# Cross-attention over 32 batches: the first four batches of x added, measured and normalised one at a time, the second quad added by DMA, early turns of x behind scores

## The chip, the cores and the metric

The kernel runs on one NeuronCore of a Trainium2 chip. Such a core has five engines that run their own instruction queues in order and wait for one another through semaphores: TensorE (matrix products and transposes; PE in the profile, PEld its weight loads), VectorE (DVE), ScalarE (ACT), GpSimd (POOL) and SyncE (SP, which here only issues DMAs). The metric is the device time of one execution in microseconds (us).

## The reference

The inputs are x and ctx, both (32, 256, 256) in fp32, and the weights of two layers. What is computed, cut to what matters:

```python
# layer 0: 16 heads of 16 columns; only batch 0 of the attention is used
att  = softmax(heads(x[0] @ Wq.T) @ heads(ctx[0] @ Wk.T).T / 4) @ heads(ctx[0] @ Wv.T)
x    = x + att                            # the one (256, 256) result is added to all 32 batches
# layer 1, for each batch
nX   = layernorm(ctx) * w1 + b1
nF   = layernorm(x) * w2 + b2
a    = softmax(nF @ nX.T / 16) @ nX       # cross-attention
c    = gelu(a @ fc1.T + fc1_b) @ fc2.T + fc2_b      # through 4 hidden columns
n    = layernorm(c) * w3 + b3
s    = softmax(n @ n.T / 16) @ n          # self-attention
out  = nF + gamma2 * (c + gamma1 * s)
```

## The kernel before, in words

The 32 batches are worked in eight quads of four (QB = 4). A batch is kept as 128 partitions x 2 rows x 256 columns (NC = 2 rows of tokens on a partition). All of x stays in one tile, x_all; ctx comes quad by quad into tiles cq. The order of all instructions is written out by hand: the kernel's Python emits them one after the other, each engine takes its own in the order in which they were emitted, and an instruction that waits holds all that stand behind it on its engine.

First comes layer 0 in eleven calls of head_step (L527, up to about 52 us), with the preparation of ctx for quads 0 and 1 beside it: statistics (stats_c), moments (moments_c), normalisation (norm_c, on GpSimd) and transposes (turn_c). Its result is att (L404, VectorE).

Then layer 1 needs, for each batch n of x:

- **addition** of att: a VectorE addition (L638) for batches 0 to 7, in add_and_stats, or for a whole quad a DMA that accumulates into x_all, issued from GpSimd (add_attention, L561);
- **statistics** of the two rows on VectorE (stats_x, BATCH_NORM_STATS2, L188);
- **moments** (L190): on GpSimd, from the statistics of several rows at once, seven small instructions and one power of -1/2 (L203), which give the scale rs and the shift nmr;
- **normalisation** in place (norm_x, L259): row 0 on GpSimd (L262), row 1 on ScalarE (L264);
- **turn** (turn_x, L568): four transposes on TensorE (L179), then two copies with scale and bias on ScalarE (L572), which give nfT;
- **score** (cross_scores, L585): eight products on TensorE (L590), their maximum on VectorE (L598), two exponentials on ScalarE (L601), which give e.

Before the loop the first eight batches get their additions and statistics (L641 to L657), with three sets of moments on GpSimd (batches 0 and 1, 2 and 3, 4 to 7) between them; values and values_turned make g_sl, which later weighs the attention, from quads 0 and 1 of ctx. Then first_step (L682) runs once for every step s, one batch a step: it transposes the exponentials of batch s - 2 (cross_turned), takes the statistics of x 8 batches ahead and of ctx 12 ahead, makes the moments of a quad of x and the next quad of ctx together at the quad's last step (moments_both), turns x of batch s + 1, normalises x of batch s + 4, turns and normalises ctx of batches s + 4 and s + 8, and makes the score of batch s. Four calls of add_attention (quads 4 to 7) stand at the first step of a quad; two (quads 2 and 3) stand before the loop. From step 20 on the second half of layer 1 is mixed in.

## Time and profile before

| | |
|---|---|
| times of three runs | 259.34, 260.54, 263.97 us; median 260.54 |
| profiled execution | 260.04 us, its span (first to last instruction) 258.3 us |
| mean granted TensorE clock | 0.967 |
| busy, share of the span | TensorE 88%, VectorE 67%, ScalarE 56%, GpSimd 72% |
| chain that ended last, by engine | TensorE 63%, GpSimd 15%, VectorE 12%, ScalarE 3% |
| 52 to 60 us | TensorE 4.86 of 8.00 us busy, VectorE 7.80, ScalarE 3.65, GpSimd 6.97 |
| 60 to 68 us | TensorE 7.23, VectorE 7.62, ScalarE 3.34, GpSimd 7.31; clock 0.79 |
| 68 to 76 us | TensorE 6.17, VectorE 3.35, ScalarE 6.03, GpSimd 7.57; clock 0.79 |
| 92 to 130 us | TensorE 38.00 of 38.00 us, VectorE 28.29, ScalarE 27.93, GpSimd 37.05 |

The busy shares are means over stages that differ. The chain of work that ended last is followed back from the last instruction: at each step it names what released it, so it tells which engine set the pace in which stretch. A row of the timeline gives the start and the length of an instruction (or of several alike), its engine, line and tiles, and in brackets how long the engine had been idle before it and what it waited for. A busy TensorE isn't TensorE at its peak: with half the clock the same products take longer.

### The profile page before, as it was taken

The page shows a single profiled execution, that of the slowest core. Times are in us where ns is not written, and L with a number is a line of the kernel's source. Part 1 is how long each engine was busy: PE and PEld are TensorE (multiplying, and loading weights), DVE is VectorE, ACT ScalarE, POOL GpSimd, SP SyncE. Part 2 cuts the span into 40 slices and gives each one's busy share as a digit, 9 for nine tenths or more (in the row PEclk, how much of TensorE's full clock was granted, in tenths as well). Part 3 has the DMA queues.
Part 4 walks back from the last instruction along what each step waited for, and adds up shares of the span by engine and source line. Part 5 has one row for each costly group of instructions (what it writes and reads, how often), then busy time and mean ns, then how long its engine had stood idle before and what let it go on. Part 6 is the DMA issues. An engine that isn't in the chain of part 4 may idle for free.

```text
span 258.3 us, 4919 instructions
## 1 busy us (share of the span) xinstructions
PE 226.9 (88%) x1797; PEld 167.3 (65%) x1797; DVE 171.8 (67%) x371; ACT 144.4 (56%) x297; POOL 185.6 (72%) x298
## 2 busy tenths in 40 slices
PE   3878989977699999999999999989999699899960
PEld 3655666645487787978888796666666356565530
DVE  1369669799738587776868565465445567877482
ACT  1126454444686787677858984656743655454610
POOL 7006827989999989999958989992419808999200
PEclk9999999997979999999999999999999979999995
DMA  6859997059398766718000000000000024343466
GB/s 204 279 190 381 384 388 278 4 100 192 63 241 221 125 202 114 213 28 141 0 3 0 0 3 0 4 0 0 0 3 0 4 81 162 123 159 132 161 237 256
DMA packets 17526, 32.76 MB, mean 127 GB/s; under 512 B 1175, under 2 KB 2142, under 8 KB 17502
## 3 DMA queue, kind: packets, MB, share of 16 engines
q1 hardware_dynamic: 12462, 23.28, 24.8%
q0 software_dynamic: 3168, 6.29, 14.7%
q10 hardware_dynamic: 1872, 2.88, 3.1%
q8 instruction: 14, 0.23, 0.4%
q14 instruction: 10, 0.08, 0.1%
HBM read 17.73 MB, written 8.39 MB: 101 GB/s over the span
## 4 chain that ended last, share of the span: by engine, by line
PE 63%; POOL 15%; DVE 12%; ACT 3%; issue 3%; DMA 1%; DVEq 0%; ACTq 0%; POOLq 0%
PE sc L590 19%; PE sc L368 9%; PE pt_x L179 5%; PE pt_c L179 4%; PE pt_e L179 4%; PE pv L282 3%; PE pu L282 3%; PE po L368 3%; POOL rs_x L203 2%; POOL r L777 2%; PE pf L282 2%; PE pp L321 2%; POOL cq L255 2%; PE ph L282 2%; DVE x_all L934 1%
## 5 line engine op out<-in xcount | busy, mean ns | idle before, releaser
L590 PE MATMUL sc<-nxT,nfT 128*128 128x256 f32 x256 | 64.3, 396 | 0.3 <-ACT nfT L572 0.3
L590 PEld LDWEIGHTS sc<-nxT,nfT 128*128 128x128 f32 x256 | 47.9, 197 | 11.5 <-issue 4.9
L598 DVE TENSOR_REDUCE nm<-sc 128x2 f32<-128x512 f32 x32 | 22.1, 691 | 37.1 <-PE sc L590 20.7
L601 ACT ACTIVATE e<-sc,nm 128x256 f32<-128x256 f32 x64 | 26.8, 470 | 26.1 <-DVE nm L598 26.1
L581 POOL TENSOR_TENSOR x_all<-x_all,w_bc 128x512 f32<-128x512 f32 x32 | 39.6, 1275 | 0.0
L572 ACT ACTIVATE nfT<-pt_x,bq,wq 128x256 f32<-128x256 f32 x64 | 33.3, 582 | 0.0
L179 PE MATMUL pt_x<-ident,x_all 128*128 128x128 f32 x132 | 21.3, 287 | 8.4 <-DMA x_all<-in_x_dram 4.3
L255 POOL TENSOR_SCALAR cq<-cq,rs_b,nmr_b 128x256 f32<-128x256 f32 x40 | 24.8, 708 | 0.0
L188 DVE BATCH_NORM_STATS2 st<-x_all 128x6 f32<-128x256 f32 x64 | 23.9, 415 | 0.3
L179 PEld LDWEIGHTS pt_x<-ident,x_all 128*128 128x128 f32 x132 | 16.2, 147 | 9.4 <-POOL wkT L153 4.2
L179 PE MATMUL pt_e<-ident,e 128*128 128x128 f32 x128 | 20.0, 276 | 2.6 <-ACT e L601 2.5
L356 ACT ACTIVATE e_h<-sc_h,nm_h 128x256 f32<-128x256 f32 x32 | 12.6, 475 | 17.1 <-DVE nm_h L351 17.1
L179 PE MATMUL pt_c<-ident,cq 128*128 128x128 f32 x132 | 20.5, 280 | 1.6 <-DVE ut L801 0.8
L275 DVE COPY nxT<-pt_c 128x512 f32<-128x512 f32 x28 | 19.0, 677 | 4.1 <-PE pt_c L179 4.1
L368 PE MATMUL po<-w_out,vt 32*128 32x256 f32 x128 | 17.9, 412 | 3.4 <-DVE vt L808 2.2
L934 DVE TENSOR_TENSOR x_all<-po,x_all 128x512 f32<-128x512 f32 x26 | 16.7, 684 | 6.0 <-PE po L368 4.2
L188 DVE BATCH_NORM_STATS2 st<-cq 128x6 f32<-128x256 f32 x56 | 20.7, 411 | 0.0
L179 PEld LDWEIGHTS pt_e<-ident,e 128*128 128x128 f32 x128 | 15.4, 141 | 7.3 <-ACT e L601 3.9
L608 ACT COPY eTq<-pt_e 128x512 f32<-128x512 f32 x32 | 18.7, 587 | 1.9 <-PE pt_e L179 1.8
L368 PE MATMUL sc<-tt,ut 32*128 32x256 f32 x128 | 19.4, 403 | 0.0
L368 PE MATMUL sc<-ut 32*128 32x256 f32 x128 | 19.4, 413 | 0.0
L179 PEld LDWEIGHTS pt_c<-ident,cq 128*128 128x128 f32 x132 | 15.5, 143 | 3.6 <-DVE ut L801 1.0
(190 smaller groups left out, 464.9 us busy)
## 6 DMA issues: line engine op xcount, KB each, us to landing
out_dram<-x_all SPq DMA_DIRECT2D x16, 512.0 KB
x_all<-in_x_dram SPq DMA_DIRECT2D x6, 1024.0 KB
x_all<-att POOLq DMA_DIRECT2D x6, 1024.0 KB, 9.2
cq<-in_ctx_dram SPq DMA_DIRECT2D x5, 1024.0 KB
cq<-in_ctx_dram ACTq DMA_DIRECT2D x2, 1024.0 KB
x_all<-in_x_dram SPq DMA_DIRECT2D x1, 1792.0 KB
cq<-in_ctx_dram SPq DMA_DIRECT2D x1, 768.0 KB
wq_nat<-in_L_xattn_Wq_dram ACTq DMA_DIRECT2D x1, 256.0 KB
```

Source lines behind the costliest of these rows:

```text
L179: nc.tensor.transpose(pt[:, dc, t * P : (t + 1) * P], src[:, t, dc * P : (dc + 1) * P], ident)
L188: nc.vector.bn_stats(st[:, t, :], src[:, t, :])
L255: nc.gpsimd.tensor_scalar(row, row, rs[:, i + t, :], nmr[:, i + t, :], ALU.mult, ALU.add)
L275: copy(nxT_of[q][:, b], turned(cq_of[q][:, b], "tp", f"c_{n}"))
L282: nc.tensor.matmul(pg[SL * b : SL * (b + 1), 0, :], weights(kc, b), moving[:, b, kc, :], start=(kc == 0), stop=(kc == NC - 1),)
L368: nc.tensor.matmul(dst[i][:, t, :], lhs[r : r + SL, t * P : (t + 1) * P], rhs[r : r + SL, :], start=True, stop=True,)
L572: nc.scalar.activation(nfT_of[n][:, dc, :], px[:, dc, :], AF.Identity, bias=bq[:, dc : dc + 1], scale=wq2[:, dc : dc + 1],)
L581: nc.gpsimd.tensor_mul(x_all[:, n], x_all[:, n], w2_bc.unsqueeze(1).to_broadcast([P, NC, D]))
L590: nc.tensor.matmul(sc[:, qt, :], nfT[:, dc, qt * P : (qt + 1) * P], nxT[:, dc, :], start=(dc == 0), stop=(dc == NC - 1),)
L598: nc.vector.tensor_reduce(nm, sc, AX.X, ALU.max, negate=True)
L601: nc.scalar.activation(e[:, qt, :], sc[:, qt, :], AF.Exp, bias=nm[:, qt : qt + 1])
L934: nc.vector.tensor_add(x_all[:, n], po[i], x_all[:, n])
```

## The change

The first eight batches are prepared in another way. For batches 0 to 3, add_first does one batch at a time: addition, statistics, then five of the seven small instructions of the moments on VectorE, the power on GpSimd, the statistics of one batch of ctx (11 to 14) on VectorE, and the last two small instructions (product) on VectorE again. Both rows of these four batches are normalised on ScalarE. Batches 4 to 7 are added by DMA (add_attention of the second quad, the first after att), and their statistics and moments come in steps 1 and 2 of the loop, two batches at a time, with the small instructions on VectorE too. Those of batches 8 to 11 come in step 3. The DMA addition of quad 2 stands behind batch 0, those of quads 3 and 4 in steps 0 and 1. In steps 0 to 2 the turn of the next batch of x stands behind the score on TensorE, and ahead of the maximum and the exponentials; the copy of the turn of c7 on ScalarE stands behind the rows of batch 1. From step 4 on the steps are as before.

```diff
@@ -187,28 +187,35 @@
         for t in range(NC):
             nc.vector.bn_stats(st[:, t, :], src[:, t, :])
 
-    def moments(st, n, name):
-
+    def moments(st, n, name, eng=None):
+
+        eng = eng or nc.gpsimd
 
         def t(what, c=1, bufs=2):
             return small.tile([P, n, c], F32, tag=f"{what}{n}", name=f"{what}_{name}", bufs=bufs)
 
         sm, df, sq, v4, ve, nm = t("sm", 2), t("df"), t("sq"), t("v4"), t("ve"), t("nmean")
         rs, nmr = t("rs", 1, 3), t("nmr", 1, 3)
-        nc.gpsimd.tensor_sub(df, st[:, :, 1:2], st[:, :, 4:5])
-        nc.gpsimd.tensor_add(sm, st[:, :, 1:3], st[:, :, 4:6])
-        nc.gpsimd.tensor_mul(sq, df, df)
-        nc.gpsimd.tensor_scalar(v4, sm[:, :, 1:2], 4.0 / D, 4 * EPS, ALU.mult, ALU.add)
-        nc.gpsimd.tensor_add(ve, v4, sq)
+        eng.tensor_sub(df, st[:, :, 1:2], st[:, :, 4:5])
+        eng.tensor_add(sm, st[:, :, 1:3], st[:, :, 4:6])
+        eng.tensor_mul(sq, df, df)
+        eng.tensor_scalar(v4, sm[:, :, 1:2], 4.0 / D, 4 * EPS, ALU.mult, ALU.add)
+        eng.tensor_add(ve, v4, sq)
         nc.gpsimd.tensor_tensor(
             rs.rearrange("p n o -> p (n o)"),
             ve.rearrange("p n o -> p (n o)"),
             neg_half[:, 0:n],
             ALU.pow,
         )
-        nc.gpsimd.tensor_scalar(nm, sm[:, :, 0:1], -0.5, 0.0, ALU.mult, ALU.add)
-        nc.gpsimd.tensor_mul(nmr, nm, rs)
-        return rs, nmr
+
+        def product():
+            eng.tensor_scalar(nm, sm[:, :, 0:1], -0.5, 0.0, ALU.mult, ALU.add)
+            eng.tensor_mul(nmr, nm, rs)
+
+        if eng is nc.gpsimd:
+            product()
+            return rs, nmr
+        return rs, nmr, product
 
     neg_half = const.tile([P, 2 * TQ], F32)
     nc.gpsimd.memset(neg_half, -0.5)
@@ -240,6 +247,16 @@
         rn = moments(flat(st_of[q][:, 1, lo:hi]), (hi - lo) * NC, f"x{q}_{lo}")
         for b in range(lo, hi):
             mx_of[q * QB + b] = *rn, (b - lo) * NC
+
+    def first_moments(lo, hi):
+
+        q, a, b = lo // QB, lo % QB, (hi - 1) % QB + 1
+        rs, nmr, product = moments(
+            flat(st_of[q][:, 1, a:b]), (hi - lo) * NC, f"x{q}_{a}", nc.vector
+        )
+        for n in range(lo, hi):
+            mx_of[n] = rs, nmr, (n - lo) * NC
+        return product
 
     def moments_both(q):
 
@@ -258,12 +275,14 @@
 
     def norm_x(n):
         rs, nmr, i = mx_of.pop(n)
-        row = x_all[:, n, 0, :]
-        nc.gpsimd.tensor_scalar(row, row, rs[:, i, :], nmr[:, i, :], ALU.mult, ALU.add)
-        row = x_all[:, n, 1, :]
-        nc.scalar.activation(
-            row, row, AF.Identity, bias=nmr[:, i + 1, :], scale=rs[:, i + 1, :]
-        )
+        for t in range(NC):
+            row = x_all[:, n, t, :]
+            if t == 0 and n >= QB:
+                nc.gpsimd.tensor_scalar(row, row, rs[:, i, :], nmr[:, i, :], ALU.mult, ALU.add)
+            else:
+                nc.scalar.activation(
+                    row, row, AF.Identity, bias=nmr[:, i + t, :], scale=rs[:, i + t, :]
+                )
 
 
     nxT_of, nfT_of, col_of, eT_of, e_of = {}, {}, {}, {}, {}
@@ -594,12 +613,16 @@
                     start=(dc == 0),
                     stop=(dc == NC - 1),
                 )
-        nm = small.tile([P, NC], F32, tag="nm", name=f"nm_{n}")
-        nc.vector.tensor_reduce(nm, sc, AX.X, ALU.max, negate=True)
-        e = wk.tile([P, NC, D], F32, tag="e", name=f"e_{n}", bufs=6)
-        for qt in range(NC):
-            nc.scalar.activation(e[:, qt, :], sc[:, qt, :], AF.Exp, bias=nm[:, qt : qt + 1])
-        e_of[n] = e
+
+        def softmax():
+            nm = small.tile([P, NC], F32, tag="nm", name=f"nm_{n}")
+            nc.vector.tensor_reduce(nm, sc, AX.X, ALU.max, negate=True)
+            e = wk.tile([P, NC, D], F32, tag="e", name=f"e_{n}", bufs=6)
+            for qt in range(NC):
+                nc.scalar.activation(e[:, qt, :], sc[:, qt, :], AF.Exp, bias=nm[:, qt : qt + 1])
+            e_of[n] = e
+
+        return softmax
 
     def cross_turned(n):
         q, b = n // QB, n % QB
@@ -631,36 +654,31 @@
         nc.vector.tensor_copy(n_all[:, q], g[:, :, :, 0:NM])
 
 
-    for q in range(2, 4):
-        add_attention(q * QB, (q + 1) * QB)
-
-    def add_and_stats(n):
+
+    def add_first(n):
         nc.vector.tensor_add(x_all[:, n], x_all[:, n], att)
         stats_x(n)
-
-    add_and_stats(0)
-    add_and_stats(1)
-    moments_x(0, 0, 2)
+        ends = first_moments(n, n + 1)
+        stats_c(11 + n)
+        ends()
+
+    add_attention(QB, 2 * QB)
+    add_first(0)
     turn_c(4, nc.scalar.copy)
     turn_c(5, nc.scalar.copy)
     values(0)
-    add_and_stats(2)
-    add_and_stats(3)
     turn_c(6, nc.scalar.copy)
+    norm_x(0)
+    add_attention(2 * QB, 3 * QB)
+    add_first(1)
+    values_turned(0)
+    turn_x(0)
+    norm_x(1)
     turn_c(7, nc.scalar.copy)
-    values_turned(0)
-    norm_x(0)
-    norm_x(1)
-    moments_x(0, 2, 4)
     values(1)
-    for n in range(4, 8):
-        add_and_stats(n)
-    turn_x(0)
+    add_first(2)
+    norm_x(2)
     values_turned(1)
-    norm_x(2)
-    norm_x(3)
-    stats_c(11)
-    moments_x(1, 0, 4)
     moments_c(2)
     l0_stage.close()
     late = ctx.enter_context(tc.tile_pool(name="late", bufs=1, reuse_waits="tile"))
@@ -683,23 +701,34 @@
         q, b = s // QB, s % QB
         if b == 0 and 2 <= q and q + 4 < NQ:
             load_c(q + 4)
-        if b == 0 and q + 4 < NQ:
+        if s < 2:
+            add_attention((3 + s) * QB, (4 + s) * QB)
+        elif b == 0 and q + 4 < NQ:
             add_attention((q + 4) * QB, (q + 5) * QB)
         if 0 <= s - 2 < B:
             cross_turned(s - 2)
-        if s + 2 * QB < B:
+        if 0 < s < QB:
+            lo, hi = ((4, 6), (6, 8), (8, 12))[s - 1]
+            for n in range(lo, hi):
+                stats_x(n)
+            if s < QB - 1:
+                first_moments(lo, hi)()
+        elif s >= QB and s + 2 * QB < B:
             stats_x(s + 2 * QB)
-        if s + 3 * QB < B:
+        if s == 2:
+            stats_c(15)
+        elif s >= QB and s + 3 * QB < B:
             stats_c(s + 3 * QB)
         if b == QB - 1 and q + 2 < NQ:
             if q + 3 < NQ:
                 moments_both(q + 2)
             else:
                 moments_x(q + 2, 0, QB)
-        if s + 1 < B:
+        if QB - 1 <= s < B - 1:
             turn_x(s + 1)
-        if s + QB < B:
-            norm_x(s + QB)
+        for n in {0: (), 1: (3,), 2: (4, 5), 3: (6, 7)}.get(s, (s + QB,)):
+            if n < B:
+                norm_x(n)
         if s + QB < B and s >= QB:
             turn_c(s + QB)
         if s + 2 * QB < B:
@@ -720,7 +749,12 @@
         for f, *args in between:
             f(*args)
         if s < B:
-            cross_scores(s)
+            softmax = cross_scores(s)
+            if s < QB - 1:
+                turn_x(s + 1)
+            softmax()
+        if s == 0:
+            add_first(3)
         if s in (0, 2):
             load_c(QB + s // 2, queue=nc.scalar)
```

## The prediction

> **What bounds the kernel now.** I read the table of 40 slices first. TensorE is at nine tenths nearly throughout, with a hole between slices 8 and 11 (52 to 77 us), where its clock is also below full. The edit lies in that hole, so I read the chain of work that ended last, in order of time, there:

> ```profile
> 57.26 1.04 POOL rs_x L203
> ...
> 62.23 1.54 POOL rs_x L203
> ...
> 66.63 1.65 POOL rs_x L203
> ...
> 71.54 3.00 PE sc L590 x8
> ...
> 75.42 1.73 PE sc L590 x8
> ...
> 87.20 1.92 PE sc L590 x8
> ```

> Columns: start, length, engine, tile and line. Until 68 the chain runs over three powers (L203) on GpSimd, each ahead of the normalisation of some batches of x. From 71.5 it runs over the scores (L590). By the timeline scores 0 to 7 start at 61.71, 65.88, 71.33, 75.25, 78.29, 81.33, 87.13, 90.49. Scores 0 and 2 take 2.9 and 3.2 instead of 1.9: PEclk is 7 in slices 9 and 11, and 9 elsewhere here.

> What is late at score 6 decides what the edit is worth, since from 87 to 149 the chain is nearly all TensorE. Any shift of score 6 goes on to the end: the one long GpSimd wait there is for VectorE, which waits for TensorE:

> ```profile
> 136.26 0.24 POOL L198 TENSOR_TENSOR df_b<-st 128x16 f32<-128x16 f32 x1 [3.67 <-DVE st L188]
> ```

> The pieces that the edit moves, in the timeline (start, length, engine, line, tiles, count):

> ```profile
> 52.30 0.69 DVE L638 TENSOR_TENSOR x_all<-x_all,att 128x512 f32<-128x512 f32 x1
> ...
> 56.50 0.68 POOL L202 TENSOR_TENSOR ve_x<-v_x,sq_x 128x4 f32<-128x4 f32 x1
> 57.26 1.04 POOL L203 TENSOR_TENSOR rs_x<-ve_x,neg_half 128x4 f32<-128x4 f32 x1
> ...
> 66.25 0.74 DVE L188 BATCH_NORM_STATS2 st<-x_all 128x6 f32<-128x256 f32 x2
> ...
> 72.00 1.34 POOL L562 DMA_DIRECT2D x_all<-att  x1
> ...
> 79.32 2.92 POOL L203 TENSOR_TENSOR rs_b<-ve_b,neg_half 128x16 f32<-128x16 f32 x1
> ```

> To be seen: a VectorE addition is 0.69, the statistics of one batch 0.66 to 0.74, a DMA addition holds GpSimd for 1.3, a power takes 1.04 for 4 elements and 2.92 for 16 (1.65 for 8 above), so 0.158 per element.

> **Taken away.** Four VectorE additions (4 x 0.69); 21 small GpSimd instructions (three sets of 7, about 1.6 a set) and three powers (1.04 + 1.54 + 1.65); four GpSimd row normalisations (0.54 each).

> **Added.** Six sets of 7 small instructions on VectorE, six powers on GpSimd, four row normalisations on ScalarE (0.55 each, hidden: ScalarE is 3.4 of 8 busy from 60 to 68), one DMA addition. No row shows these small operations on VectorE. The nearest: 0.14 (addition 128x4, L450), 0.20 (reciprocal, L403), 0.29 (product 128x128, L404); start to start 0.24 where one needs the one before (42.29 to 42.53) and 0.13 where not. I take 0.95 for a set of five and 0.2 for a last product. A power of 2 elements isn't shown: 0.72 on the line through the three, with 0.5 and 1.04 as ends.

> **The walk.** I pass the changed order of instructions through the four in-order queues with these lengths. The same walk over the order of before gives scores 61.8, 66.7, 71.3, 74.8, 77.9, 80.9, 87.4: within 0.9 of the trace everywhere, 0.3 late at score 6. The changed order:

> Batch 0: att is ready at 52.26; addition, statistics, five small to 54.7; power to 55.5, product 55.8; ScalarE's two rows to 56.9. The turn of x0 starts at 56.9, against 59.66: 2.7 earlier. That gain is lost at once. Batch 1's addition stands behind batch 0's product on VectorE, so its rows end at 60.3; only then does ScalarE copy the turn of c7, which values(1) needs (0.9 to 61.8), whose copy and turn (to 62.6) stand before score 0 on TensorE. Score 0: 62.6, against 61.7.

> Batch 3: GpSimd takes batch 2's power to 62.6, then, before batch 3's, moments_c(2) (3.3, to 65.9), the third DMA addition (1.3, to 67.1) and two rows of norm_c (1.5 with a short wait, to 68.6). Power to 69.3. VectorE, in batch 3's product since 69.3, goes on at 69.5.

> Behind that product stand on VectorE: statistics of batches 4 and 5 (1.4) and five small (0.9), 71.8; a wait for their power (71.9 to 72.9, behind the fourth DMA addition, which ended at 70.6); product 73.1; only now the maximum of score 1 (0.68, 73.8), though score 1 ended at 68.8. Again for batches 6 and 7: 1.4 + 0.9 to 76.1, power to 77.1, product 77.3, statistics of c15 (0.66), maximum of score 2 to 78.7. Who waits: the exponentials of scores 1 and 2, the transposes of e1 and e2, and, as the rows of x4 stand behind the second power on GpSimd (78.2), the turn of x4 and score 3 (78.1, against 75.25).

> Then VectorE does statistics of batches 8 to 11 (2.7, to 81.35). GpSimd starts moments_both(2) there: 1.05 small, 2.92 power, 0.5, to 85.85. **Batch 6's row stands behind it** (86.4; before it stood ahead). Turns of x6 and c9, 0.9: score 5 at 87.3, against 81.33. Then e4, x7, c10 (1.3), pv (1.0) and score 5 itself (1.73): score 6 at 91.3, against 87.1: **+4.2**.

> **DMA.** Landing takes 8.9 to 14.3. The second quad's addition (quad 1 in the code), issued at 52.6, lands by 66.9 at worst, and is read at 69.5; quad 2's, issued at 55.5, by 69.8, and is read at 78.7. Both are hidden; a later landing would cost VectorE the difference one for one. Quads 3 and 4 are issued at 65.8 and 69.3, and read from step 4 (84) and step 8 on. The ctx loads on ScalarE's queue keep their distance to their readers.

> [...] GpSimd's row at 56.50 takes 0.68 instead of 0.20, and the power at 62.23 1.54 instead of 1.04, each beginning with a VectorE addition (L638 at 56.45 and 62.23). [...] Four additions fewer then free GpSimd of about 4 x 0.5 = 2.0 by the rows; the walk lets it wait for VectorE from 70.6 on, so this buys nothing there.

> The reciprocal of 8 elements takes 0.20, the addition of 512 0.69: 64 times the work for 3.5 times the time. [...]

> **Sum.** The profiled run took 260.04, its span 258.3 and 1.74 around it; it is 0.5 under the median 260.54. 258.3 + 4.2 + 1.74 = **264.2**, 1.4% over that median.

> Ends of the unknown terms on the chain: 15 small pieces at 0.14 to 0.29 instead of 0.19: -0.7 to +1.5; two powers of 4 at 1.04 to 1.54: 0 to +1.0; batch 3's power: -0.2 to +0.3; a DMA issue at 1.27 to 1.82 (the longest row): 0 to +0.5; 18 statistics at 0.33 to 0.37: 0 to +0.7; the walk's own lateness in before: -0.3; a half clock at score 5 or 6, as score 2 had (3.2 for 1.9): 0 to +1.3. Together 263.0 to 269.5; not all at once: 262.5 to 266.3.

> **Rivals.**
> 1. The same mechanism with the dear ends (contended powers, half clock behind the longer TensorE waits): 266 to 269. For it: both half-clock stretches of before followed waits of TensorE, and this walk has longer ones, 73.9 to 77.7 and 83.7 to 86.4. Against: scores 2 to 4 can take a half clock for nothing, as VectorE is later still.
> 2. Not slower: GpSimd reaches batch 3's power early. [...] The point that decides is whether VectorE goes on from batch 3's product before 65.5 or near 69.5. For it: GpSimd's rows here were lengthened by collisions, and four additions go. Against: the order puts 6 us of work, by uncontended rows of 3.3, 1.3 and 1.1, before that power.
> 3. Nothing comes of it: the shift is given back after 91, 259.5 to 261.5. For it: GpSimd is 37.05 of 38.0 busy from 92 to 130, and could be the bound that absorbs a late TensorE. Against: TensorE is 38.0 of 38.0 busy there, and GpSimd then idles 3.67.

> **How the numbers follow.** Forecast 0.62 (262.5 to 266.3), rival 1 0.17, rival 2 0.13, rival 3 0.08. The range 259.8 to 267.2 leaves out most of rival 2 and the upper part of rival 1, some 0.18. About 2% (255.3 to 265.8) is what a measurement of this kernel can tell from no change. Above 265.8: rival 1 and a tenth of the forecast, 0.24. Below 255.3: 0.03, beyond rival 2's end. Between: 0.73.

> **What would show it.** Scores 0 to 6 near 62.6, 66.9, 71.6, 78.1, 81.4, 87.3, 91.3; the turn of x0 near 57; the maximum of score 1 on VectorE over 3 us after its score has ended; VectorE's longest waits in this stage released by the power; a POOL moments_both(2) from 81 to 86 with score 5 behind it; from score 6 on the rows of before, 4 later. It is wrong if batch 3's power runs before 66, if score 5 doesn't wait for batch 6's row, or if the shift at score 6 isn't there at the end.

## The result, and the profile after

The changed kernel took 267.22 us (median of 265.57 to 268.01), the kernel before beside it 262.25 (259.34 to 264.54); the ratio, explained below, is 1.028 with an interval of 1.024 to 1.032. It is slower, as the steps of the forecast have it, but by more: the forecast was 264.2, and the time lies just above the end of its range (259.8 to 267.2).

The same chain of waits as shown of before, now of the changed kernel (start, length, engine, tile and line):

```profile
70.68 0.72 POOL rs_x L204
...
73.67 1.04 POOL rs_x L204
...
77.62 1.01 POOL rs_x L204
...
84.05 2.91 POOL rs_b L204
...
87.45 0.55 POOL x_all L281
...
90.02 2.44 PE sc L609 x8
...
94.76 1.93 PE sc L609 x8
```

Before, the chain left the powers at 68 and ran over scores from 71.5. Now it goes through three more powers, the last of 16 elements, and only at 88 through the row of batch 6 to score 5. The pieces behind that, from the timeline of the changed kernel (in brackets the idle time ahead, and what ended it):

```profile
54.49 0.69 DVE L659 TENSOR_TENSOR x_all<-x_all,att 128x512 f32<-128x512 f32 x1
...
67.75 0.69 DVE L619 TENSOR_REDUCE nm<-sc 128x2 f32<-128x512 f32 x1 [3.08 <-PE sc L609]
...
70.68 0.71 POOL L204 TENSOR_TENSOR rs_x<-ve_x,neg_half 128x2 f32<-128x2 f32 x1 [0.74 <-DVE ve_x L203]
71.36 1.32 POOL L581 DMA_DIRECT2D x_all<-att  x1
...
74.73 0.21 DVE L213 TENSOR_TENSOR nmr_x<-nmean_x,rs_x 128x4 f32<-128x4 f32 x1 [1.08 <-POOL rs_x L204]
74.87 0.68 DVE L619 TENSOR_REDUCE nm<-sc 128x2 f32<-128x512 f32 x1
...
78.66 0.16 DVE L213 TENSOR_TENSOR nmr_x<-nmean_x,rs_x 128x4 f32<-128x4 f32 x1 [1.04 <-POOL rs_x L204]
...
88.05 1.11 PE L179 MATMUL pt_x<-ident,x_all 128*128 128x128 f32 x4 [2.83 <-POOL x_all L281]
...
143.82 0.24 POOL L199 TENSOR_TENSOR df_b<-st 128x16 f32<-128x16 f32 x1 [3.68 <-DVE st L188]
```

To be seen: VectorE stands for 1.08 and 1.04 in the last product of a set, waiting for the power; the maximum of score 1 (74.87) starts 4.05 after its score has ended (70.8), and the waits for powers are 1.24 of that, the rest is VectorE's own work, statistics above all; TensorE then waits 2.83 for batch 6's row. Not as forecast: the power of batch 3 (70.68) is released by VectorE, which had waited 3.08 for score 0, while GpSimd sat idle for 0.74. Far behind, GpSimd's wait of 3.67 is still there (3.68): nothing absorbs the shift.

Executions of both kernels lie in two groups some 4 us apart, and each ratio leaves out executions over 1.5% above the fastest beside them, so that 1.028 sets 267.22, of the changed kernel's upper group, against the lower group of the kernel before alone (259.34 and 260.54). Of 101 executions of the kernel before 77 were near 259.5 and 23 near 264 (one more took 298.56, at a mean clock of 0.743), of 14 of the changed kernel 4 near 263.5 and 10 near 267.5. So the changed kernel was profiled three times. Times from the profiles, us (the last column is the span less the start of score 6):

| profile | attention ready | score 5 after it | score 6 after it | from there to the end |
|---|---|---|---|---|
| before | 52.26 | 29.1 | 34.87 | 171.1 |
| changed, first (267.54) | 54.46 | 35.35 | 40.23 | 170.95 |
| changed, second (263.26) | 51.83 | 34.36 | 38.50 | 171.0 |
| changed, third (267.49) | 54.31 | 35.36 | 40.24 | 170.95 |

The first and the third differ from the second in two places that reach score 6, and both are the clock. Windows of the first (stretch, length, busy us of PE, PEld, DVE, ACT and POOL with counts, granted clock, DMA share, GB/s):

```profile
22.00:24.00 2.00, 2.00 (x16) 1.67 (x13) 1.92 (x3) 0.14 (x1) 1.84 (x3) 0.77 1.05 399
24.00:26.00 2.00, 2.00 (x10) 1.49 (x10) 1.24 (x4) 1.90 (x5) 1.68 (x9) 0.50 1.07 391
26.00:28.00 2.00, 2.00 (x16) 0.69 (x18) 1.07 (x1) 0.00 (x0) 2.00 (x4) 0.50 1.02 381
...
88.00:90.00 2.00, 1.95 (x9) 1.96 (x10) 0.00 (x0) 2.00 (x6) 2.00 (x4) 0.50 0.00 0
90.00:92.00 2.00, 2.00 (x8) 1.65 (x7) 0.69 (x1) 0.77 (x2) 2.00 (x4) 0.67 0.35 59
```

and the same of the second:

```profile
22.00:24.00 2.00, 2.00 (x18) 1.67 (x18) 1.92 (x4) 0.48 (x2) 1.85 (x3) 1.00 1.06 405
24.00:26.00 2.00, 1.69 (x20) 0.73 (x18) 1.95 (x4) 1.56 (x4) 1.75 (x8) 1.00 1.06 390
26.00:28.00 2.00, 2.00 (x19) 1.37 (x10) 0.50 (x2) 1.57 (x4) 2.00 (x5) 1.00 1.04 384
...
86.00:88.00 2.00, 2.00 (x13) 1.75 (x12) 0.69 (x1) 1.91 (x5) 2.00 (x4) 1.00 0.00 0
```

A half clock between 23 and 30, ahead of every instruction that the change touches, makes the attention 2.5 to 2.6 later; in all four profiles on record that have it the attention is ready at 54.3 to 54.5, in the thirteen without at 51.3 to 52.7. One on the turn of batch 6 and score 5 makes score 6 later by 1.6: from batch 6's row to score 6 it is 6.7 in the first profile (88.00 to 94.69) and 5.1 in the second (85.22 to 90.33). What is left goes with the order: **score 6 starts 3.6 later after the attention** (38.50 against 34.87). These two profiles aren't free of half clocks either. In that of the kernel before score 2 takes 3.21 instead of 2.0 on the chain; in the second of the changed kernel score 3 takes 3.54 instead of 1.89, but TensorE waits for batch 6's row behind it all the same (1.28).

### The profile page after: what moved, and what is told of

Its sections match the earlier page's. It is cut to its first block, busy times and chain, and to the rows that moved or that the text cites. A ratio compares the mean times of both kernels' runs of the same rounds, so it can differ in the third digit from the quotient of the medians.

```text
span 265.6 us, 4946 instructions
## 1 busy us (share of the span) xinstructions
PE 230.1 (87%) x1797; PEld 169.3 (64%) x1797; DVE 173.7 (65%) x409; ACT 146.9 (55%) x301; POOL 180.4 (68%) x277
## 3 DMA queue, kind: packets, MB, share of 16 engines
q0 software_dynamic: 3696, 7.34, 16.3%
## 4 chain that ended last, share of the span: by engine, by line
PE 59%; DVE 19%; POOL 12%; issue 3%; ACT 3%; DMA 1%; DVEq 0%; POOLq 0%; ACTq 0%
PE sc L609 18%; PE sc L387 8%; PE pt_x L179 4%; PE pt_c L179 4%; DVE st L188 4%; PE pt_e L179 4%; PE po L387 3%; PE pv L301 3%; PE pf L301 2%; PE pu L301 2%; POOL rs_x L204 2%; POOL r L811 2%; DVE x_all L968 2%; PE pp L340 2%; POOL cq L272 2%
## 5 line engine op out<-in xcount | busy, mean ns | idle before, releaser
L619 DVE TENSOR_REDUCE nm<-sc 128x2 f32<-128x512 f32 x32 | 22.1, 689 | 35.3 <-PE sc L609 19.1
L591 ACT ACTIVATE nfT<-pt_x,bq,wq 128x256 f32<-128x256 f32 x64 | 33.1, 577 | 3.9 <-PE pt_x L179 3.9
L188 DVE BATCH_NORM_STATS2 st<-x_all 128x6 f32<-128x256 f32 x64 | 23.3, 412 | 0.1
L179 PE MATMUL pt_c<-ident,cq 128*128 128x128 f32 x132 | 21.1, 284 | 1.2 <-DVE ut L835 0.8
L188 DVE BATCH_NORM_STATS2 st<-cq 128x6 f32<-128x256 f32 x56 | 20.7, 411 | 0.0
L387 PE MATMUL sc<-tt,ut 32*128 32x256 f32 x128 | 19.3, 402 | 0.0
L179 PEld LDWEIGHTS pt_e<-ident,e 128*128 128x128 f32 x128 | 15.4, 141 | 4.5 <-ACT e L622 1.2
```

The source lines that it names most:

```text
L179: nc.tensor.transpose(pt[:, dc, t * P : (t + 1) * P], src[:, t, dc * P : (dc + 1) * P], ident)
L188: nc.vector.bn_stats(st[:, t, :], src[:, t, :])
L387: nc.tensor.matmul(dst[i][:, t, :], lhs[r : r + SL, t * P : (t + 1) * P], rhs[r : r + SL, :], start=True, stop=True,)
L591: nc.scalar.activation(nfT_of[n][:, dc, :], px[:, dc, :], AF.Identity, bias=bq[:, dc : dc + 1], scale=wq2[:, dc : dc + 1],)
L619: nc.vector.tensor_reduce(nm, sc, AX.X, ALU.max, negate=True)
```

## The experiments

Theory: the forecast's line. The early powers on GpSimd, waited for by VectorE in its own order, hold the maxima of scores 1 and 2 and the statistics of batches 8 to 11, and batch 6's row, put behind moments_both(2), is the last link ahead of score 5. Rivals: one of the parts does it by itself (the DMA addition's landing, or the turns behind the scores); the shift isn't the order's but the clock's.

### One part at a time, in the kernel before

**The rows of batches 0 to 3 on ScalarE**, nothing else:

```diff
-        row = x_all[:, n, 0, :]
-        nc.gpsimd.tensor_scalar(row, row, rs[:, i, :], nmr[:, i, :], ALU.mult, ALU.add)
...
+        for t in range(NC):
+            row = x_all[:, n, t, :]
+            if t == 0 and n >= QB:
+                nc.gpsimd.tensor_scalar(row, row, rs[:, i, :], nmr[:, i, :], ALU.mult, ALU.add)
+            else:
+                nc.scalar.activation(
...
```

> The kernel before with one part of the change alone: both rows of batches 0 to 3 are normalised on ScalarE. Theory (the order on GpSimd and VectorE decides, walked with the rows of before): GpSimd is free of four rows of 0.54, moments_both of batches 8 to 11 starts earlier, and score 6 starts 33.2 us after att is ready instead of 34.9, so the time is 1.7 to 1.9 under before. Rival (TensorE alone decides here, what GpSimd does is hidden): no difference, score 6 at 34.9.

Measured: score 6 33.03 after the attention, 1.8 earlier than in the kernel before, as the theory had it; the time 259.32, a ratio of 0.999 (0.995 to 1.004). The theory's time, 1.7 to 1.9 less, is missed. In the profile half of the 1.8 is given back: attention at 52.74 (0.5 later) and 171.6 from score 6 to the end (0.5 more); the span is 0.9 shorter. At score 6 this part is a gain, not the loss; in the times no difference can be told.

**The second quad by DMA**, with the later two DMA additions in steps 0 and 1 as the change has them, the statistics left where they were:

```diff
-    for q in range(2, 4):
+    for q in range(1, 3):
         add_attention(q * QB, (q + 1) * QB)
...
-        add_and_stats(n)
+        stats_x(n)
...
-        if b == 0 and q + 4 < NQ:
+        if s < 2:
+            add_attention((3 + s) * QB, (4 + s) * QB)
+        elif b == 0 and q + 4 < NQ:
```

> The kernel before with the second part alone: batches 4 to 7 are added by DMA (the first DMA addition), their statistics stay where they were, the additions of quads 3 and 4 move to steps 0 and 1. Theory: no gain and no loss at score 6 (34.9 to 35.2 after att), since moments_both keeps its place; time within 0.5 of before. Rival (the DMA addition and its landing are what costs in the change): 2 to 4 later, VectorE waiting at the statistics of batch 4 for the landing.

Measured: score 6 38.26, 3.4 later, and 262.65, a ratio of 1.008 (1.004 to 1.012). The theory missed; the rival holds. VectorE's waits from 50 to 92 (in total, times, longest):

```profile
DVE st L188 <- DMA x_all<-att: 9.3, 3, 5.1
```

It stood 9.3 us for the landing of three additions that took 9.2 to 13.9; a half clock on score 5 (3.20 instead of 1.89) is part of the 3.4. In the changed kernel no wait of VectorE for a DMA is in the list: there batch 4's statistics come 17.0 after the attention, behind batch 3's product. So the part is dear alone and hidden in the whole; parts measured alone can't be added up.

**The turns of x1 to x3 behind the scores:**

```diff
-        if s + 1 < B:
+        if QB - 1 <= s < B - 1:
             turn_x(s + 1)
...
-            cross_scores(s)
+            softmax = cross_scores(s)
+            if s < QB - 1:
+                turn_x(s + 1)
+            softmax()
```

> The kernel before with the third part alone: in steps 0 to 2 the turn of the next batch of x stands behind the score on TensorE, ahead of maximum and exponentials. Theory: score 1 starts some 3 to 4 later after att (its turn waits for score 0), but score 6 only 0.1 to 0.8 later (35.0 to 35.7), since the row of batch 8 behind moments_both is later still. Rival (the turns cost the change its time): 2 to 4 later at score 6 too.

Measured: score 1 starts 17.6 after the attention (13.6 before), TensorE waiting 5.2 for the turn's copy on ScalarE; but score 6 is only 1.25 later (36.12), and the time is 259.55, a ratio of 1.000 (0.996 to 1.004). Most of the 4.0 of score 1 is made up for by score 6, though 1.25 is more than the theory's 0.8. In the profile the 1.25 doesn't reach the end, since the attention was ready 0.7 earlier and the rest took 170.2.

**The small operations of the first three sets of moments on VectorE:**

```diff
-    def moments(st, n, name):
+    def moments(st, n, name, eng=None):
+        eng = eng or nc.gpsimd
...
-        nc.gpsimd.tensor_sub(df, st[:, :, 1:2], st[:, :, 4:5])
+        eng.tensor_sub(df, st[:, :, 1:2], st[:, :, 4:5])
...
+            nc.vector if q < 2 else nc.gpsimd,
```

> The kernel before with the fourth part alone: the seven small instructions of the first three sets of moments (batches 0 and 1, 2 and 3, 4 to 7) on VectorE, the power on GpSimd, all in the old places. Theory (VectorE, held in each last product by the power, keeps additions, statistics and maxima behind it waiting): score 2 at 23.0 after att instead of 19.1, score 6 at 37.1 instead of 34.9, time 2.0 over before. Rival (small instructions on VectorE are cheap and only relieve GpSimd): score 6 1 to 2 earlier.

Measured: 263.21, a ratio of 1.012 (0.999 to 1.025, which doesn't exclude no change); score 2 23.1 after the attention and score 6 37.91, 3.0 later. VectorE's waits from 50 to 92:

```profile
DVE nmr_x L211 <- POOL rs_x L204: 3.8, 3, 1.7
```

This is the wait that the change adds, alone: three times VectorE stands in a last product for a power of 1.0 to 1.7. Score 2 starts 4.0 later after the attention than in the kernel before (19.1), and that is before its half clock (3.62 instead of 2.0), which the kernel before has too (3.21). The profile also has the half clock from 23 to 30 and the attention at 54.49, with the head of the kernel before unchanged.

### The named link: batch 6's row

The changed kernel with the rows of batches 6 and 7 ahead of moments_both(2):

```diff
+        if s == QB - 1:
+            norm_x(6)
+            norm_x(7)
         if b == QB - 1 and q + 2 < NQ:
...
-        for n in {0: (), 1: (3,), 2: (4, 5), 3: (6, 7)}.get(s, (s + QB,)):
+        for n in {0: (), 1: (3,), 2: (4, 5), 3: ()}.get(s, (s + QB,)):
```

> The changed kernel with the rows of batches 6 and 7 put ahead of the second quad-pair's moments in step 3; all else as in the changed kernel. In the changed kernel's profile the row of batch 6 ends at 88.05 on GpSimd, behind five small operations and a power of 2.91 us for those moments (84.05), and score 5 starts 35.35, score 6 40.23 after the attention is ready. Theory (batch 6's row behind the moments is the last link at score 5): score 5 comes 2.2 us earlier, at 33.1 after the attention; score 6, whose weights then wait for other rows, 0.8 to 2.0 earlier, at 38.2 to 39.4; time 265.2 to 266.4 against 267.2. Rival (the row is not what score 5 waits for, the late thing is the second layer's rows behind the power): score 5 where it was, and the power 2.1 later, so score 6 at 41 to 42 and a time 1 to 2 above the changed kernel's.

Measured: 262.82, a ratio of 1.015 (1.008 to 1.022); score 5 33.54 after the attention (theory 33.1), score 6 38.48 (38.2 to 39.4). The time is under the theory's 265.2 to 266.4; three of its four executions are near 262.6 and one is 265.99, against 263.5 and 267.5 in the changed kernel's two groups. Its timeline:

```profile
78.86 1.09 POOL L281 TENSOR_SCALAR x_all<-x_all,rs_x,nmr_x 128x256 f32<-128x256 f32 x2
...
82.15 2.91 POOL L204 TENSOR_TENSOR rs_b<-ve_b,neg_half 128x16 f32<-128x16 f32 x1
...
85.00 1.89 PE L609 MATMUL sc<-nxT,nfT 128*128 128x256 f32 x8
```

The row ends before the power starts, and score 5 follows score 4 after 3.04, without the wait. The link is shown for score 5. At score 6 the comparison depends on the profile taken: 1.75 earlier than in the first profile of the changed kernel, level with the second (38.50). This run has a half clock of 6.8 us from 59.1, which had made its score 3 1.3 later than in the second. Counted from batch 4's row, which stands upstream of the edit, score 5 comes after 8.28 (10.36 in the second, 11.19 in the first) and score 6 after 13.22 (14.50 and 16.07): 2.1 and 1.3 gained on the second.

### VectorE's wait for the power, taken out of the changed kernel

The small operations of the early sets back on GpSimd:

```diff
-        rs, nmr, product = moments(
-            flat(st_of[q][:, 1, a:b]), (hi - lo) * NC, f"x{q}_{a}", nc.vector
+        rs, nmr = moments(
+            flat(st_of[q][:, 1, a:b]), (hi - lo) * NC, f"x{q}_{a}"
...
-        return product
+        return lambda: None
```

> The changed kernel with the small operations of the early moments (batches 0 to 7 of the first sets) back on GpSimd; all else as in the changed kernel. Theory (VectorE waits in order for each power on GpSimd, 1.08 and 1.04 us at 73.7 and 77.6, and this holds the maxima of scores 1 and 2 and so the statistics ahead of the second pair's moments): score 5 about 34.2 and score 6 about 39.1 after the attention, 1.1 earlier than the changed kernel's 35.35 and 40.23; time about 266.1. Rival (GpSimd's queue is the bound and seven more small operations a set, some 0.17 to 0.25 us each, make it longer): batch 3's power and all behind it 1 to 2 later, score 6 at 41 to 42, time 268 to 269.

Measured: 266.19, a ratio of 1.024 (1.018 to 1.030); score 6 at 41.75: the rival's figure. The run doesn't decide it cleanly, since three half-clock stretches (58.1 to 68.3, 75.2 to 78.6, 82.0 to 85.4) stand on its scores. It shows no gain from moving the small operations back; what VectorE's wait for the power costs inside the changed kernel stays open. GpSimd's operations there are also stretched beside VectorE's additions, its timeline at the first set:

```profile
54.30 1.04 POOL L200 TENSOR_TENSOR sm_x<-st 128x4 f32<-128x4 f32 x1
...
61.57 0.20 POOL L200 TENSOR_TENSOR sm_x<-st 128x4 f32<-128x4 f32 x1
```

The same operation takes 1.04 with an addition beside it and 0.20 without.

### The clock

Ten matmuls that nobody reads, in the idle place ahead of the turn of batch 6, then four, then four in each of three idle places, and the changed kernel as it is:

```diff
+        if s in (QB - 1, QB + 1):
+            filler(4)
         if QB - 1 <= s < B - 1:
             turn_x(s + 1)
...
+    filler(4)
     values(1)
...
+    def filler(n):
+        warm = sm_bank("warm")
+        for k in range(n):
+            nc.tensor.matmul(warm[:, 0, :], ident, w2_bc, start=True, stop=True)
```

(The first two have only step QB + 1, with 10 and 4.)

> The changed kernel with ten matmuls 128x128 by 128x256 that nobody reads, put in TensorE's queue ahead of the turn of batch 6 in step 5, where TensorE sat idle from 85.3 to 88.0; extra work, all else as in the changed kernel. In the changed kernel's profile the clock granted from 88.0 to 91.3 is 0.50, and score 5 takes 2.65 us. Theory (the idle stretch is what brings the half clock, and the half clock is the 1.2 us by which score 6 came later than the forecast's +4.2): clock 1.0 from 86 to 92, score 5 about 1.9 us long, score 6 at 39.0 after the attention against 40.23, time 266.0. Rival (the half clock comes whatever TensorE did before, or the filler only fills the queue): score 6 at 40.2 to 40.8, time 267.2 to 267.8.

Measured: 267.32, a ratio of 1.029 (1.022 to 1.036); score 6 43.88 after the attention: neither (the time is the rival's figure, but not for its reason). The edit was mis-sized. Each of these matmuls shows as two passes (x20 for ten), so ten took 4.48, and the turn behind them started 3.9 after batch 6's row had ended (86.44):

```profile
86.03 4.48 PE L730 MATMUL warm<-w_bc,ident 128*128 128x256 f32 x20
90.35 0.60 PE L179 MATMUL pt_x<-ident,x_all 128*128 128x128 f32 x4
```

> The changed kernel with four matmuls that nobody reads (each two passes of 0.216 us by the run with ten, 1.73 us in all, where ten took 4.3 and ran 3.5 past the row) ahead of the turn of batch 6 in step 5. Theory (an idle stretch of TensorE of 2 us and more is followed by a stretch at half clock, a shorter one is not): TensorE idle under 1.2 us ahead of that turn, the clock 1.0 from there to score 6, score 5 about 1.9 long, and from the start of score 4 to the start of score 6 10.4 to 10.8 us against 11.8 in the changed kernel; time 1.0 to 1.4 less than the changed kernel's of the same call. Rival (the half clock comes regardless of the idle stretch): the clock falls to 0.5 between score 4 and score 6 all the same, 11.5 to 12 us, time the same.

Measured: 265.04, a ratio of 1.023 (1.016 to 1.030). No half clock from score 4 to score 6, 8.9 us instead of 11.8. But the second profile of the changed kernel, without filler, has 8.7 there and no half clock either, after an idle stretch of only 1.3. So this run doesn't tell the two theories apart. The turn behind the filler started 0.3 after the row had ended, and the time is no gain: the changed kernel beside it took 263.49.

> The changed kernel with four matmuls that nobody reads (1.73 us) in each of the three places where TensorE sat idle for about 2 us: ahead of the products of the second quad's values (1.98), ahead of the turn of batch 4 (2.15) and ahead of the turn of batch 6 (1.3 to 2.8). In the second profile of the changed kernel the half-clock stretches of 3.4 us begin 0.3 to 0.6 after the first and the second of these. Theory (a stretch at half clock follows where TensorE was idle for about 2 us): no half clock from 56 to 92, scores of 1.9 to 2.0 us throughout, score 6 at 37.5 to 38.5 after the attention against 38.50 and 40.23 in the two profiles of the changed kernel, time at or under the changed kernel's lower executions, 261.5 to 263. Rival (the half clock comes by its own period, whatever TensorE does): one or two stretches of 3.4 us between 56 and 92 all the same, score 6 at 38.5 to 40.5.

Measured: 263.08 (262.45 to 264.76), a ratio of 1.015 (1.012 to 1.019); score 6 at 38.11. Of the three stretches that were filled none is followed by a half clock. One half-clock stretch is left, from 69.1 to 72.5, and it stands behind the one long idle stretch that was not filled, ahead of score 2:

```profile
66.28 0.60 PE L179 MATMUL pt_e<-ident,e 128*128 128x128 f32 x4
69.20 3.63 PE L609 MATMUL sc<-nxT,nfT 128*128 128x256 f32 x8 [2.32 <-ACT nfT L591]
```

The theory's "none from 56 to 92" is missed by that one, and the rival had one stretch coming all the same; but where it stands, and score 6 under the rival's 38.5, fit the theory. One profile doesn't settle it. The first two scores, behind filled places, take 1.89 and 2.02.

> The changed kernel once more, for a second profile. Its first profile has a granted clock of 0.50 to 0.77 from 22 to 30 us, ahead of every instruction that the change touches, and the attention ready at 54.46, 2.2 later than in the kernel before; the kernel before with the small operations on VectorE had the same stretch (0.83, 0.50, 0.50, 0.50 from 22 to 30) and 54.78. Theory (that stretch comes in some executions of any of these kernels, so it is no part of the change): where it is absent, the attention is ready at 51.4 to 52.6, score 6 starts 39 to 40.3 after it as the changed order sets it, and the span is 262.5 to 264; where it is present, 54.5 and about 265.6 again. In both, score 6 to the end takes 170.5 to 171.3. Rival (the change itself makes the attention late): 54.5 with a full clock from 22 to 30, or the attention early and the span 265.6 all the same.

Measured: 263.49, a ratio of 1.014 (1.008 to 1.021); no half clock from 22 to 30, the attention at 51.83, span 261.3, score 6 38.50: the theory.

> The changed kernel for a third profile and more times. Theory (the order costs 3.6 us at score 6 and the rest of what was measured first are half-clock stretches that come in some executions): executions from 262 to 268 with more than one cluster, median 263 to 266, ratio 1.014 to 1.025; row of batch 6 33.4 to 33.6 after the attention; score 6 38.5, or about 40.2 if a half-clock stretch falls on score 5; from score 6 to the end 171.0. Rival (the first set of times was the kernel's own and the second was lucky): median near 267.2, ratio near 1.028.

Measured: 267.60 (263.67 to 268.45), a ratio of 1.025 (1.019 to 1.032); its profile repeats the first, half clock from 22.9 to 29.7 included. The third row of the table stands within 0.01 of the first after the attention. The median is near the rival's 267.2, the ratio at the end of the theory's range, and score 6 and what follows it are the theory's. So the ratio of the first set was no accident of that set.

> The kernel before once more, for a second profile. The changed kernel's executions lie in two groups, near 263 and near 267.5, and its profiles in the second group have the half clock from 23 to 30 us, the attention 2.6 later and a half-clock stretch on score 5. Theory (the two groups are the place of the half-clock stretches and belong to both kernels, and the change adds 3.6 in each): executions of the kernel before near 259.3 and near 263.8; a profile in the upper group shows the half clock between 22 and 31 and the attention ready at 54.3 to 54.8, one in the lower group the attention at 51.3 to 52.8; score 6 34 to 36.5 after it, 171 from there to the end. Rival (the change alone opens the kernel to the upper group): the attention 51 to 53 in every profile of the kernel before, and its executions above 263 are late somewhere behind score 6.

> The kernel before a third time, as the run beside it: two groups of executions near 259.3 and near 263.8; in an upper one the half clock between 22 and 31 and the attention ready at 54.3 to 54.8; in a lower one 51.3 to 52.8; the rival as there.

Measured: 259.51 and 259.75, ratios of 1.000 and 0.999 to the kernel before beside them; attention at 51.84 and 51.51, score 6 34.86 and 34.94 after it, 171.1 and 171.25 to the end. Both profiles fell into the lower group. That the kernel before has an upper group too (23 of 101 executions, near 264) is seen from the times; what its profile looks like is not shown. Two variants of it with the same head, the small operations on VectorE and the version below, do have the half clock at 23 and the attention at 54.5 and 54.4, which speaks against the rival.

### A version that beats both

The kernel before with both rows of batches 0 to 6 on ScalarE (the first diff, with `n >= QB + 3`):

> The kernel before with both rows of batches 0 to 6 on ScalarE instead of one row each on GpSimd; nothing else is changed. Theory (GpSimd's queue in the early steps sets when the first scores come, and what is gained there is carried to the end as the loss was): score 6 about 31.7 after the attention against 34.87 in the kernel before, time 3 us less, near 256.5. Rival (ScalarE takes the rows' place as the bound, or the gain is used up by the steps behind score 8): score 6 at 32 to 34, time 258.5 to 260.

Measured: 257.33, a ratio of 0.990 (0.986 to 0.995) to the kernel before. Score 6 is 31.50 after the attention, 3.4 earlier, and the gain arrives at the end (170.5 from there). Its executions lie in two groups too, three near 256.3 and three near 258.25; the profile is of the upper one, with the attention at 54.37. The chain that is left, in order of time:

```profile
66.92 1.65 POOL rs_x L203
...
70.17 1.65 POOL rs_c L203
...
72.29 1.34 POOL x_all L564
73.63 3.21 POOL cq L255 x6
...
78.72 1.73 PE sc L592 x8
```

To shorten it, the context's statistics and moments were put ahead of the additions of batches 4 to 7:

```diff
+    stats_c(11)
+    moments_c(2)
     for n in range(4, 8):
         add_and_stats(n)
...
-    stats_c(11)
     moments_x(1, 0, 4)
-    moments_c(2)
```

> The kernel before with both rows of batches 0 to 6 on ScalarE, and the statistics of context batch 11 with the third context quad's moments put ahead of the additions of batches 4 to 7 instead of behind their moments. Theory (in the profile of the version with the rows alone, the chain to score 4 runs through batches 4 to 7's moments, then the context's, then an addition by DMA and six rows of context on GpSimd, which sat idle for 1.74 ahead of the first of these): the context's rows 1.5 earlier, score 4 0.5 to 0.9 earlier since TensorE then is the bound, score 6 at 30.6 to 31.0 after the attention against 31.5, time 0.5 to 0.9 under that version's 257.3. Rival (VectorE's statistics in that place make batches 4 to 7's rows later): score 3 or 4 0.5 to 1.5 later, time 258 to 259.

Measured: 258.63, a ratio of 0.998 (0.995 to 1.001): the rival. Score 6 is 33.61 after the attention. Batch 4's rows come 16.95 after it instead of 14.70, and ScalarE, which has them ahead of the exponentials of score 0, waits 3.75 for them; score 2 is 2.2 later.

## Why the prediction was right and wrong

- **The line of the walk holds in its figures.** In the second profile scores 0 to 6 start 10.58, 14.03, 18.60, 25.10, 29.83, 34.36 and 38.50 after the attention; the forecast's, less its 52.26, are 10.3, 14.6, 19.3, 25.8, 29.1, 35.0 and 39.0. The +4.2 at score 6 measured +3.6.
- **Rival 2's deciding point fell on the forecast's side.** Batch 3's power starts 16.1 to 16.2 after the attention (forecast 68.6, which is 16.3), VectorE goes on at 17.0 to 17.1 (17.2). But the forecast's reason, GpSimd's work queued ahead of that power, isn't what set it. GpSimd had ended that work 15.4 to 15.5 after the attention and sat idle for 0.67 to 0.74 until VectorE's operations of batch 3 came, and these stood behind the maximum of score 0, for which VectorE had waited 2.0 to 3.1. The forecast had the power's end and VectorE's arrival at the same 69.3, so that the figure came out is in part luck.
- **One sign did not come.** VectorE's longest waits in this stage are for score 0 (3.1) and for a turn of ctx (3.0 in the first profile); its three waits for a power are 2.3 together. The line behind batch 3 is mostly VectorE's own work in its order, with those waits in it.
- **Rival 3 is false.** From score 6 to the end it is 170.9 to 171.3 in the six profiles of the two kernels. In the variants it goes with the clock: 170.2 to 170.5 in the three without a half-clock stretch from 200 to 220 us, 172.2 in the one where that stretch is 6.8 long, 170.9 to 171.6 in the others, where it is 3.4.
- **The DMA is hidden**, as forecast; alone, without the order that hides it, it costs 3.4 at score 6, 1.3 of that beside a half clock.
- **The small operations were taken too dear.** A set of five took 0.64 in the changed kernel (56.01 to 56.65), not 0.95; a power of two elements 0.70 to 0.73, near the 0.72 taken from the line through the three others. moments_both(2) started 28.2 to 28.3 after the attention instead of 29.1, which is most of why 4.2 measured 3.6. 0.64 for five is 0.13 each, and one operation takes 0.15 to 0.17.
- **The step that failed is the sum.** It put 4.2 on the profiled run's own 258.3, and with that took two things over. First, "a half clock at score 5 or 6: 0 to +1.3" was an end of the range and not a term: it measured 1.6 in two of three profiles. Rival 1 named it, with its reason, the longer waits of TensorE ahead of it, but was given 0.17. Second, the clock of the head, 2.2 to 2.6 at the time when the attention is ready, was held to be the same because no instruction there is changed. 258.3 + 2.2 + 5.4 (40.23 less 34.87: the 3.6 and the half clock) - 0.2 behind score 6 make the 265.6 of the first profile within rounding; 258.3 - 0.4 + 3.6 - 0.2 make the 261.3 of the second, whose time, 263.26, is 0.9 under the forecast.
- **So the line behind batch 3 was right, and the size was off by the clock.** Lower group against lower group, some 259.5 and 263.5, and upper against upper, some 264 and 267.5, the change costs 4.0 and 3.5. The rest of the 1.028 is that the changed kernel fell into the upper group far more often (10 of 14, by sets of times 4 of 4, 1 of 4 and 5 of 6, against 23 of 101) and was set against the lower group, and the forecast had no term for that. Why it does so, with a head that is the same instruction for instruction, and whether it would over many more executions, stays open.

## What to carry to other kernels

Before a small operation is moved to the engine with time to spare, look at what it waits for: an engine that works in order and waits for another's power holds all that is queued behind it, here the maxima that TensorE's next work hangs on (waits of 1.08 and 1.04 in the changed kernel, 3.8 in three waits with the small operations alone on VectorE). Move work off the queue that the chain runs through without adding a wait in return (the rows on ScalarE: -1.0%), and test a part in the order it will stand in, since the same DMA addition cost 3.4 alone, and in the whole VectorE never waited for it. When idle stretches of TensorE grow to 2 us, give the half clock behind them a price in the sum (here those of 1.90 and 2.83 in the kernel before, and of 1.98 and 2.83 in the first profile of the changed kernel, each came with 3.41 at a clock of 0.50), and take more than one profile before a difference of 1% is explained.

## What the runs showed of the hardware

Whether the head gets its half clock went, in these profiles, with where those multiples fall. TensorE has an idle stretch of 0.9 near 20 us in all of them (from 20.57 in the kernel before, from 20.49 in the first profile of the changed kernel). In the four profiles with the half clock at 23 it starts 2.6 to 2.8 behind the start of that stretch (23.07 in the first of the changed kernel, 2.6 behind). In the thirteen without, a start counted back from the measured ones in steps of 3.41 would lie 1.3 to 2.3 behind it, an estimate (in the kernel before 60.34 less 11 steps is 22.83, 2.3 behind). What decides it is not shown.

Idle stretches of TensorE of 1.9 to 2.8 often came with a half-clock stretch: 2.83 and 1.90 long in the kernel before (half clock from 60.34 and 70.58), 1.98 and 2.83 in the first profile of the changed kernel (from 64.03 and 87.92). One of 2.1 to 2.2 ahead of the turn of batch 4 did in the second profile of the changed kernel and not in the first (2.15) and the third; no half-clock stretch from 50 us on starts behind idle stretches of 1.5 or less alone (1.52 ahead of score 2 in the first profile, with none).
